# Layer 3 of a four-layer convolution network on one core: from halves to quarters of the channels

## The chip, the cores and the metric

The kernel runs on one core of one Trainium2 chip. Its time is device microseconds, the median of the runs. The core has a matrix engine (TensorE, PE in the profile, with its weight loads as PEld), a vector engine (VectorE, DVE), an activation engine (ScalarE, ACT), a general engine (GpSimd, POOL) and a queue engine (SyncE, SP) that here only issues transfers. Sixteen DMA engines move data between the main memory and the on-chip memory of 128 partitions. TensorE writes to PSUM, from which VectorE and ScalarE read.

## The reference

x has 16 images of 64 x 64 pixels with 256 channels, all in float32. Four layers follow one another, each x = x + layer(groupnorm(x)). Layer 0 is a linear attention, layer 1 a gated attention over channels and space with a scan, layer 2 an involution of 3 x 3, layer 3 an involution of 7 x 7. The change concerns layer 3 and what feeds it:

```
def _L3_conv_ref(x, w_reduce, gamma, beta, mean, var, w_span, b_span):
    K = 7; G = 16
    r = jnp.einsum('bhwc,cd->bhwd', x, w_reduce)
    r = jax.nn.relu((r - mean) * (gamma / jnp.sqrt(var + BN_EPS)) + beta)
    kgen = jnp.einsum('bhwd,de->bhwe', r, w_span) + b_span
    kgen = kgen.reshape(B, H, W, G, K * K)
    ...
    patches = jnp.stack([xp[:, i:i + H, j:j + W, :] for i in range(K) for j in range(K)], axis=3)
    patches = patches.reshape(B, H, W, K * K, G, Cg)
    out = jnp.einsum('bhwgk,bhwkgc->bhwgc', kgen, patches)
```

Each pixel has its own 49 weights for each of 16 groups of 16 channels. They are computed from the pixel (256 channels to 64, then to 784) and multiplied with the 7 x 7 neighbourhood.

## The kernel before

The four layers run one after the other over all images, each with pools of its own; images go between them through tensors in main memory.

Layer 2 (lines 882 to 1284) is written in an order by hand. One turn of its loop works on an eighth of an image for each of four tasks, which lie 0, 12, 20 and 33 turns behind (LAG): the end of layer 1, the projection, the involution itself, and `centred` (line 1174). The involution runs in 128 of the 161 turns. It writes its result as x3_d (tokens by channels, line 1136) and c3_d (channels by tokens). `load_centred` and `centred` take an eighth of x3_d back in the tile xc ([P, 8, P]: 8 rows of pixels and 128 channels, two buffers), subtract the channel means on POOL, and store it in sixteen transfers to `strips`. That tensor holds, for each half h of the channels, the padded image in eight strips of 14 columns (8 and three on each side), so that 9 rows of a strip are 126 consecutive rows. A turn's stores are issued in the following turn, all on SP; only in the last turns every second one goes by ACT (line 1229). The zero rows and columns of `strips` are written in layer 0, in `entered` (line 237), once an image.

Layer 3 (lines 1288 to 1492) goes over images, halves h of 128 channels, and eleven turns td. Here the framework's planner may move instructions on an engine, within what the data permits. At td = 0 `matrices(h)` (line 1353) makes four tiles wm, each for 32 channels, that is two groups: PE multiplies the spread weights `span` with the reduced pixels rt into a PSUM tile pk (three in turn, shared with pa), and ACT (line 1379, four instructions) or DVE (line 1384, one) adds the bias and moves it to wm. Five of twelve tiles go to ACT. Each wm has 126 rows, the places of a tile of 9 x 14 inputs, and for each of 176 tiles of 3 x 8 outputs 2 x 24 columns. There are four wm buffers, all in use by one half.

`involution7` (line 1420) is one turn: two rows of tiles, k, and eight tiles in each. For each tile four matmuls, one for each wm, multiply xw (the patches, 126 x 32) with wm into 32 partitions each of pa. Both groups' kernels are applied to all 32 channels; the instructions on ACT (line 1437) and DVE (line 1438) then take the right one with the mask msk and the norm's factor. `finished` (line 1443) transposes the turn before back to tokens on PE, adds the residual ot and stores it.

`load_patches` loads two xw of 512 KB (six buffers), two turns ahead; `load_residual` loads ot one turn ahead (three buffers). In a half with h = 1, each turn also reduces a part of the next image: `load_reduced` and `reduced` (line 1323), with four matmuls and three instructions on ACT. All transfers of layer 3 are issued on SP.

Of the kernel before, what the change touches and what calls it, by code (L numbers as in the profile page):

```python
# [44 lines left out]
def network(ctx: ExitStack, tc: tile.TileContext, a: dict, out: bass.AP):  # L45
# [21 lines left out]
    gmat = const("gmat", [P, P], a["gmat"])  # L67
    ones = const("ones", [P, P])
    nc.vector.memset(ones, 1.0)
# [24 lines left out]
    strips = dram.tile([NI, 2, HW + 9, TC + 6, NTC, P], F32, tag="strips", name="strips")  # L94
# [89 lines left out]
    with ExitStack() as st:  # L184
# [22 lines left out]
        hsum = aconst("hsum", [P, 4], a["hsum"])  # L207

# [28 lines left out]
        def entered(i, ch):  # L237

            if ch == 0:

                for h in range(2):
                    for r0, n in ((0, 3), (67, 6)):
                        nc.sync.dma_start(
                            out=strips[i, h, r0 : r0 + n].rearrange("r w t c -> (r w) (t c)"),
                            in_=a["zero"][0 : n * (TC + 6), :],
                        )
                    for tj, c0 in ((0, 0), (NTC - 1, TC + 3)):
                        nc.sync.dma_start(
                            out=strips[i, h, 3:67, c0 : c0 + 3, tj, :],
                            in_=a["zero"][0:HW, 0 : 3 * P].rearrange("r (w c) -> r w c", w=3),  # L250
                        )
# [630 lines left out]
    with ExitStack() as st:  # L882
# [61 lines left out]
        def load_centred(i, rc):  # L944
            q, h = divmod(rc, 2)
            x3n = x3_d[i].rearrange("(g r w) c -> g w r c", g=2, w=HW)
            load("xc", [P, 8, P], *(
                (
                    lambda t, g=g: t[g * HW : (g + 1) * HW],
                    x3n[g][:, q * 8 : q * 8 + 8, h * P : (h + 1) * P],  # L950
# [223 lines left out]
        def centred(i, rc):  # L1174


            q, h = divmod(rc, 2)
            xc = taken("xc")
            mean = gmb[i][:, h * P : (h + 1) * P]
            nc.gpsimd.tensor_tensor(  # L1180
                xc, xc, mean.unsqueeze(1).broadcast_to([P, 8, P]), ALU.subtract
            )
            for g in range(2):
                r0 = 3 + 32 * g + 8 * q
                for tj in range(NTC):
# [3 lines left out]
                        strips[i, h, r0 : r0 + 8, c0 : c0 + hi - lo, tj, :].rearrange(  # L1189
# [98 lines left out]
    with ExitStack() as st:  # L1288
        pc = st.enter_context(tc.tile_pool(name="c_const", bufs=1))
        wk = st.enter_context(tc.tile_pool(name="c_work", bufs=2))  # L1290
        wm_p = st.enter_context(tc.tile_pool(name="c_wm", bufs=4))
# [9 lines left out]
        wr3 = cconst("wr3", [P, 2, 64], a["w_reduce"].rearrange("(h p) f -> p h f", p=P))  # L1301
        wr3t = cconst("wr3t", [P, 2, 2, 64])
        for k in range(2):
            nc.vector.tensor_copy(wr3t[:, :, k, :], wr3)
# [48 lines left out]
        def matrices(h):  # L1353
# [3 lines left out]
            for q in range(4):  # L1357
                w = wm_p.tile([P, NTL, 2 * TILE_OUT], F32, tag="wm", name="wm")
                wm.append(w)
                for n in range(12):  # L1360
# [3 lines left out]
                    for m in range(2):  # L1364
                        for b in range(2):
# [5 lines left out]
                                lhsT=span[half, h * 8 + q * 2 + gg, s0 : s0 + P],  # L1371
# [95 lines left out]
        for n, (i, h, td) in enumerate(turns):  # L1467
# [13 lines left out]
            if td == 0:  # L1481
                wm = matrices(h)
# [118 lines left out]
```

## Time and profile before

| | us |
|---|---|
| median of 3 runs | 10119.68 (10116.0 to 10123.17) |
| profiled execution | 10143.46, its span 10141.2 |
| PE busy | 7922.7 (78%) |
| DVE busy | 6659.6 (66%) |
| ACT busy | 5277.9 (52%) |
| POOL busy | 2348.4 (23%) |
| patch matmuls, line 1428 | 45056 instructions, busy 826.8, idle before them 503.5 |
| matrix matmuls, line 1369 | 12288 instructions, busy 1186.3, idle before them 151.8 |
| bias on DVE, line 1384 | 896 of 1.343 us |
| bias on ACT, line 1379 | 2560 of 0.542 us |

Times in the views are microseconds from the start of one profiled execution. Busy time of an engine is an average over stages with different limits. A number in brackets behind an instruction is the time for which its engine stood idle before it, and what ended that; "issue" means that the profile shows no release. One matmul of the program appears as two instructions where its operands are float32. The DMA share is the mean busy share of the sixteen DMA engines.

### The profile page before, as it was taken

The numbers are of one execution on the slowest core, as the hardware profiler recorded it, in microseconds if no ns is written. First come the engines' busy times: TensorE is split into PE (matmuls) and PEld (weight loads), VectorE is DVE, ScalarE is ACT, GpSimd is POOL, SyncE is SP. The second block draws the span as 40 slices with busy tenths as digits, with TensorE's granted clock in tenths as the row PEclk, the third lists the DMA queues.
The fourth block names the chain that finished last, engine by engine and source line by source line (L and its number), as shares of the span: only waits on it lengthen the run. The fifth ranks groups of instructions, "written<-read, shape, count | busy, mean of one in ns | idle before, by whom it ended". The sixth has DMA issues, their size and how long they took to land.

```text
span 10141.2 us, 213891 instructions
## 1 busy us (share of the span) xinstructions
PE 7922.7 (78%) x85976; PEld 5657.2 (56%) x85976; DVE 6659.6 (66%) x11056; ACT 5277.9 (52%) x12544; POOL 2348.4 (23%) x1193
## 2 busy tenths in 40 slices
PE   8888888888888774777777777745787877777787
PEld 5666666666666531454554545533565656656565
DVE  4666666666666546799999999963454545545454
ACT  4555555555555436666666666533444444444444
POOL 0111111111110101567777677650000000000000
PEclk9999999999999868899889898967998888889988
DMA  7433444443343228667777777664656565555555
GB/s 244 143 131 127 136 142 140 135 133 129 127 145 115 86 82 262 203 209 229 228 229 228 228 227 229 192 152 137 206 165 196 163 203 168 180 183 183 185 163 189
DMA packets 1373248, 1762.68 MB, mean 174 GB/s; under 512 B 103649, under 2 KB 1067570, under 8 KB 1371106
## 3 DMA queue, kind: packets, MB, share of 16 engines
q1 hardware_dynamic: 1360266, 1743.26, 55.2%
q8 instruction: 679, 11.12, 0.4%
q10 hardware_dynamic: 11992, 5.74, 0.3%
q14 instruction: 311, 2.55, 0.1%
HBM read 1234.54 MB, written 536.87 MB: 175 GB/s over the span
## 4 chain that ended last, share of the span: by engine, by line
PE 33%; DVE 28%; DMA 13%; ACT 11%; issue 8%; POOL 4%; SPq 2%; ACTq 0%; DVEq 0%; POOLq 0%
DVE pd L1105 7%; PE pa L1428 7%; DVE wm L1384 6%; PE pq L296 5%; PE pk L1369 5%; PE py L452 4%; DMA x<-x_d 3%; PE pr L1337 3%; DVE x L1273 2%; DMA c_d<-c 2%; ACT sq L461 2%; ACT wm L1379 2%; DMA strips<-xc 2%; DMA xn<-x_d 2%; DVE y L457 1%
## 5 line engine op out<-in xcount | busy, mean ns | idle before, releaser
L296 PE MATMUL pq<-wq,xn 128*128 128x384 f32 x4096 | 1474.0, 499 | 62.3 <-DVE diag L345 20.9
L1105 DVE TENSOR_TENSOR pd<-xs,pw 128x576 f32<-128x576 f32 (+15 forms) x3072 | 1437.5, 546 | 8.9 <-PE pw L1059 5.5
L1369 PE MATMUL pk<-rt,span 64*128 64x176 f32 x12288 | 1186.3, 331 | 151.8 <-DVE wm L1384 60.0
L1384 DVE TENSOR_TENSOR wm<-pk,spanb 128x704 f32<-128x704 f32 x896 | 1148.3, 1343 | 229.2 <-PE pk L1369 229.2
L1428 PE MATMUL pa<-wm,xw 126*32 126x48 f32 x45056 | 826.8, 228 | 503.5 <-issue 405.8
L1369 PEld LDWEIGHTS pk<-rt,span 64*128 64x128 f32 x12288 | 949.7, 190 | 383.0 <-ACT wm L1379 181.9
L1116 POOL TENSOR_TENSOR pd<-pd 128x2048 f32<-128x2048 f32 (+2 forms) x384 | 1068.2, 2782 | 404.0 <-DVE pd L1105 383.9
L1379 ACT ACTIVATE wm<-pk,spanb 128x176 f32<-128x176 f32 x2560 | 976.2, 542 | 344.4 <-PE pk L1369 335.9
L1428 PEld LDWEIGHTS pa<-wm,xw 126*32 126x32 f32 x45056 | 686.6, 125 | 748.5 <-issue 549.2
L1438 DVE SCALAR_TENSOR_TENSOR ex<-pa,msk,ex 128x192 f32<-128x192 f32 x704 | 286.9, 415 | 1189.3 <-ACT ex L1437 1187.3
L296 PEld LDWEIGHTS pq<-wq,xn 128*128 128x128 f32 x4096 | 751.8, 193 | 495.5 <-issue 56.3
L1437 ACT ACTIVATE ex<-pa,msk 128x192 f32<-128x192 f32 x704 | 289.7, 421 | 1057.8 <-PE pa L1428 1055.1
L1075 PE MATMUL pt<-ident,pad 128*128 128x128 f32 x4608 | 637.5, 292 | 158.2 <-ACT rt L1052 54.6
L1028 PE MATMUL px<-x2p,wis 128*128 128x512 f32 x1024 | 571.5, 706 | 212.7 <-ACT c L1130 177.3
L1075 PEld LDWEIGHTS pt<-ident,pad 128*128 128x128 f32 x4608 | 540.6, 151 | 316.7 <-ACT rt L1052 66.3
L1079 ACT COPY xs<-pt 128x512 f32<-128x512 f32 x1152 | 607.8, 587 | 184.2 <-PE pt L1075 183.6
L1273 DVE TENSOR_REDUCE x<-pd 128x512 f32<-128x4608 f32 x128 | 633.3, 4948 | 1.4
L452 PE MATMUL py<-wo,oT 128*128 128x256 f32 x2048 | 486.6, 389 | 60.8 <-DVE va L312 45.2
L464 POOL TENSOR_TENSOR rsy<-ss,mhalf 128x4 f32<-128x4 f32 x128 | 130.1, 1017 | 1629.4 <-DVE ss L462 1629.4
L461 ACT ACTIVATE sq<-y 128x256 f32<-128x256 f32 x512 | 213.2, 416 | 526.0 <-DVE y L457 517.6
L1028 PEld LDWEIGHTS px<-x2p,wis 128*128 128x128 f32 x1024 | 217.4, 226 | 471.9 <-issue 230.9
L1344 ACT ACTIVATE rt<-pr,b,sb 128x128 f32<-128x128 f32 x528 | 202.0, 452 | 516.1 <-PE pr L1337 516.1
(242 smaller groups left out, 13899.4 us busy)
## 6 DMA issues: line engine op xcount, KB each, us to landing
xw<-strips SPq DMA_DIRECT2D x704, 512.0 KB
xn<-x_d SPq DMA_DIRECT2D x256, 512.0 KB
x<-x_d SPq DMA_DIRECT2D x256, 512.0 KB
x_d<-x SPq DMA_DIRECT2D x256, 512.0 KB
strips<-xc SPq DMA_DIRECT2D x1464, 56.0 KB
xin<-in_x SPq DMA_DIRECT2D x256, 256.0 KB
x_d<-xc SPq DMA_DIRECT2D x128, 512.0 KB
xm<-x_d SPq DMA_DIRECT2D x128, 512.0 KB
```

The source lines that it names most:

```text
L296: nc.tensor.matmul(pq[:, dd, 0:384], lhsT=xn[:, h, tok], rhs=wq[:, h, hf * 384 : (hf + 1) * 384], start=(h == 0), stop=(h == 1),)
L452: nc.tensor.matmul(py[:, q, :], lhsT=oT[hf][:, q * P : (q + 1) * P], rhs=wo[:, hf, :], start=(hf == 0), stop=(hf == 1),)
L1028: nc.tensor.matmul(px, lhsT=w[:, h, fh * P : (fh + 1) * P], rhs=x2[:, h], start=(h == 0), stop=(h == 1),)
L1075: nc.tensor.transpose(pt[:, k, h * P : (h + 1) * P], lines[:, h, rc * 4 + e + k, 2 * j : 2 * j + P], ident,)
L1079: nc.scalar.copy(t[:, e : e + 2, 0:C], pt)
L1105: nc.vector.tensor_tensor(pd[:, :, o - oh * P : o - oh * P + n, :], xs[dj][:, di : di + 4, c0 : c0 + 9 * n].rearrange("p r (f k) -> p r f ...
L1116: nc.gpsimd.tensor_tensor(pd[..., 0:n], pd[..., 0:n], pd[..., n : 2 * n], ALU.add)
L1273: nc.vector.tensor_reduce(x3[:, :, P:C], pd1, AX.X, ALU.add)
L1369: nc.tensor.matmul(pkv[:, b, m], lhsT=span[half, h * 8 + q * 2 + gg, s0 : s0 + P], rhs=rto[half, o, :], start=True, stop=True,)
L1379: nc.scalar.activation(dst[:, m // 2, m % 2], pkv[:, m // 2, m % 2], AF.Identity, bias=spanb[:, g0 + m : g0 + m + 1],)
L1384: nc.vector.tensor_tensor(dst, pkv, spanb[:, g0 : g0 + 4].rearrange("p (b m) -> p b m", b=2).unsqueeze(3).broadcast_to([P, 2, 2, NTL]), AL ...
L1428: nc.tensor.matmul(pav[32 * q : 32 * q + 32, :, tj * TC : (tj + 1) * TC], lhsT=xws[k][0:TILE_IN, tj, 32 * q : 32 * q + 32], rhs=wm[q][0:TI ...
```

## The change

Layer 3 goes over quarters of 64 channels (a half h and a part pr) and not over halves. For each quarter two matrices wm are made (two buffers, before four), and a turn of `involution7` puts its two rows of tiles k side by side in the partitions of one pa: 64k + 32q. A turn so has half of the matmuls that it had, one instruction on ACT and one on DVE, and there are twice as many turns. `finished` has two transposes of 96 columns.

The patches have 24 tiles xw of 4 KB a partition, each for one turn of a quarter. A quarter's eleven are loaded at the start of the quarter before. The residual ot has four buffers of 4 x 64, in blocks of 96 tokens by 64 channels. The tile that ends a quarter is handed to `finished` before the next matrices. ACT takes 4 and 5 of twelve PSUM tiles in turn.

`strips` is laid out by quarters, so xc is [P, 16, 64], 16 rows and 64 channels, and a stored or loaded piece is 64 channels long. The zero rows of all quarters go in one transfer each. The constants gmat and ones move to pools of earlier layers, wr3 is loaded straight into wr3t, and the mask is made with small matmuls.

```
-    strips = dram.tile([NI, 2, HW + 9, TC + 6, NTC, P], F32, tag="strips", name="strips")
+    strips = dram.tile([NI, 4, HW + 9, TC + 6, NTC, 64], F32, tag="strips", name="strips")
...
-                for h in range(2):
-                    for r0, n in ((0, 3), (67, 6)):
-                        nc.sync.dma_start(
-                            out=strips[i, h, r0 : r0 + n].rearrange("r w t c -> (r w) (t c)"),
-                            in_=a["zero"][0 : n * (TC + 6), :],
-                        )
+                for r0, n in ((0, 3), (67, 6)):
+                    nc.sync.dma_start(
+                        out=strips[i, :, r0 : r0 + n].rearrange("q r w t c -> q (r w) (t c)"),
+                        in_=a["zero"][:, 0 : n * (TC + 6), :],
+                    )
+                for q in range(4):
...
         def load_centred(i, rc):
-            q, h = divmod(rc, 2)
+            quarter, q = divmod(rc, 2)
...
-            load("xc", [P, 8, P], *(
+            load("xc", [P, 16, 64], *(
...
-                    x3n[g][:, q * 8 : q * 8 + 8, h * P : (h + 1) * P],
+                    x3n[g][:, q * 16 : q * 16 + 16, quarter * 64 : quarter * 64 + 64],
...
-                        strips[i, h, r0 : r0 + 8, c0 : c0 + hi - lo, tj, :].rearrange(
+                        strips[i, quarter, r0 : r0 + 16, c0 : c0 + hi - lo, tj, :].rearrange(
                             "r w c -> w r c"
...
-        wm_p = st.enter_context(tc.tile_pool(name="c_wm", bufs=4))
+        wm_p = st.enter_context(tc.tile_pool(name="c_wm", bufs=2))
+        xw_p = st.enter_context(tc.tile_pool(name="c_xw", bufs=NTR + 2))
...
-        def matrices(h):
+        def matrices(h, pr):
...
-            for q in range(4):
+            for q in range(2):
...
-                    if n % 12 in (1, 3, 6, 8, 10):
+                    if n in ((1, 4, 6, 9), (1, 3, 6, 8, 10))[q]:
...
+        TB = TR * HW // 2
...
+        def tokens(t, i, h, pr, td):
+
+            t = t[i, :, h * P + pr * 64 : h * P + pr * 64 + 64]
+            t0 = td * TR * HW
+            if t0 + 4 * TB <= NT:
+                return [t[t0 : t0 + 4 * TB].rearrange("(m p) c -> p m c", p=TB)]
...
+        def load_patches(i, quarter, td):
+
+            xw = xw_p.tile([P, 2, NTC, 64], F32, tag="xw", name="xw")
+            rows = strips[i, quarter].rearrange("r w t c -> (r w) (t c)")
+            t0, step = td * TR * (TC + 6), TR * (TC + 6)
+            for k in range(2):
                 nc.sync.dma_start(
+                    out=xw[:, k].rearrange("p t c -> p (t c)"),
+                    in_=rows[t0 + k * step : t0 + k * step + P],
+                )
+            xws[i, quarter, td] = xw
+
+        def load_residual(i, h, pr, td):
+            ot = wk.tile([P, 4, 64], F32, tag="ot", name="ot", bufs=4)
+            for dst, src in zip(blocks(ot, td), tokens(x3_d, i, h, pr, td)):
+                nc.sync.dma_start(out=dst, in_=src)
             return ot
...
+            for tj in range(NTC):
+                for k in range(2):
+                    for q in range(2):
+                        p0 = 64 * k + 32 * q
                         nc.tensor.matmul(
+                            pav[p0 : p0 + 32, :, tj * TC : (tj + 1) * TC],
+                            lhsT=xw[0:TILE_IN, k, tj, 32 * q : 32 * q + 32],
...
+            nc.scalar.activation(ex, pag[:, 0], AF.Identity, scale=msk[:, pr, h, 0:1])
+            nc.vector.scalar_tensor_tensor(
+                ex, pag[:, 1], msk[:, pr, h, 1:2], ex, ALU.mult, ALU.add
+            )
             return ex
...
+        def finished(i, h, pr, td, ex, ot):
+
+            po = sm.tile([P, 2, P], F32, tag="sm", name="po")
+            for b in range(2):
+                nc.tensor.transpose(po[0:TB, b, :], ex[:, b * TB : (b + 1) * TB], ident)
...
+            return list(zip(tokens(outs, i, h, pr, td), blocks(ot, td)))
...
             if td == 0:
+                if quarters:
+                    following = quarters.pop(0)
+                    for t in range(0, NTR, 2):
+                        load_patches(*following, t)
+                if last:
+                    for dst, src in finished(*last):
+                        nc.sync.dma_start(out=dst, in_=src)
+                    last = None
+                wm = matrices(h, pr)
+            ex = involution7(i, h, pr, td, wm, msk)
             if last:
                 store = finished(*last)
-            if h == 1 and i + 1 < NI:
+            if h == pr == 1 and i + 1 < NI:
                 reduced(i + 1, td, cs.pop((i + 1, td)))
```

## The prediction

> **What bounds it now.** I read the page first, for where the transfers are busy. One digit is 254 us. Layer 2's multiplications run from 4127 to 6749 us (digits 17 to 27, mostly 7), layer 3's matrices begin at 6956 us (digit 28 on, 5 and 6).
>
> ```profile
> DMA  7433444443343228667777777664656565555555
> ```
>
> Then the view by stretches, with two rounds of layer 3 cut into their two stages.
>
> ```profile
> 7961.00:7999.00 38.00, 33.72 (x366) 26.99 (x362) 33.43 (x28) 28.64 (x76) 0.00 (x0) 1.00 0.14 43
> 8000.00:8048.00 48.00, 34.57 (x1393) 26.77 (x1390) 14.44 (x32) 9.37 (x24) 0.00 (x0) 0.79 0.83 269
> 8050.00:8089.00 39.00, 33.95 (x364) 27.06 (x361) 34.06 (x29) 28.82 (x76) 0.00 (x0) 1.00 0.17 57
> 8090.00:8154.00 64.00, 48.92 (x1490) 33.22 (x1488) 15.88 (x38) 20.99 (x56) 0.00 (x0) 0.87 0.83 269
> ```
>
> The columns are us, then busy us and instructions of PE, weight loads, DVE, ACT and POOL, then granted clock, DMA share and GB/s. While matrices are made (38 and 39 us) the DMA share is 0.14 and 0.17; while they are used (48 us, or 64 with the next image's reduction) it is 0.83. The round is a sum of two stages with different limits: DVE, ACT and the ring of PSUM tiles in one, patches in the other. The order of time shows it in PE: it stands idle for "issue" in front of patch matmuls when buffers have run dry, and goes fast when they are full.
>
> ```profile
> 8031.73 1.23 PE L1428 MATMUL pa<-wm,xw 126*32 126x48 f32 x97 [2.15 <-issue]
> ...
> 8044.45 0.89 PE L1428 MATMUL pa<-wm,xw 126*32 126x48 f32 x64 [0.59 <-DVE ex L1438]
> 8045.27 0.33 PE L1449 MATMUL po<-ident,ex 128*128 128x128 f32 x1
> 8045.53 0.89 PE L1428 MATMUL pa<-wm,xw 126*32 126x48 f32 x64
> 8046.35 0.44 PE L1449 MATMUL po<-ident,ex 128*128 128x128 f32 x2
> ```
>
> The change also touches layer 2, which writes the strips. There DVE is bound (20.35 us a turn: two first multiplications lie at 5506.95 and 5527.30), and SP is hardly freer:
>
> ```profile
> 5505.77 9.61 SPq L1230 DMA_DIRECT2D strips<-xc  x16
> 5506.95 11.23 DVE L1105 TENSOR_TENSOR pd<-xs,pw 128x576 f32<-128x576 f32 x24
> ...
> 5517.27 1.29 SPq L926 DMA_DIRECT2D xc<-x_d  x2
> 5518.60 0.62 SPq L926 DMA_DIRECT2D x2p<-x_d  x1
> ...
> 5525.23 1.25 SPq L1230 DMA_DIRECT2D c_d<-c  x2
> ```
>
> SP spends 9.6 us on sixteen strip stores, then stands 1.9 us until they have landed, because the next xc goes into their buffer; everything else of its turn takes 8.2 us, so its loop is about 19.7 us.
>
> **The price of a packet.** Two stretches move nearly one size alone: the end of layer 2 (512-byte pieces) and layer 1's statistics (2 KB rows).
>
> ```profile
> 6800.00:6900.00 100.00, 0.00 (x0) 0.00 (x0) 0.00 (x0) 0.00 (x0) 21.04 (x9) 0.50 0.62 130
> ...
> 3830.00:3930.00 100.00, 66.66 (x112) 18.09 (x112) 78.72 (x225) 77.28 (x225) 0.00 (x0) 0.95 0.87 291
> ```
>
> The view of the DMA queues counts their packets:
>
> ```profile
> DMA packets 27686, 13.04 MB, mean 130 GB/s; under 512 B 2264, under 2 KB 27684, under 8 KB 27684
> ...
> DMA packets 15094, 29.14 MB, mean 291 GB/s; under 512 B 890, under 2 KB 890, under 8 KB 15088
> ```
>
> 0.62 x 16 engines x 100 us = 992 engine-us over 25,422 packets is 39 ns, 38 with something off for the small ones; 0.87 x 1600 over 14,204 is 98 ns. The straight line through them (0.039 ns a byte, 18 ns fixed) gives 178 ns for 4 KB, 78 for 1.5 KB, 28 for 256 B. Test on before: an image of layer 3 moves 5632 patch rows of 4 KB, 16,384 pieces of 512 B (residual in, result out) and 2816 of 1.5 KB: 1002 + 623 + 220 = 1845 engine-us, 115 us on 16 engines; the measured share is 0.56 of 198.5 us (3176 us over 16 images), 111. The line holds, but 256 B lies outside the two sizes.
>
> [...]here 64 patch instructions take 0.89 or 1.51 us, and the clock is 1.00 with matrices and 0.79 with patches.
>
> **Part by part.** Layer 3, matrices. A quarter makes 24 PSUM tiles. Before, 48 take 40.4 us (first at 6956.4, first patch matmul at 6996.8), 0.84 us each, and a changeover costs about 1.7 more (42.2 us from the last patch matmul at 8049.3 to full use at 8091.5). So a quarter: 20.3 + 1.7 = 22 us, an image 88 where it had 84. DVE gets 15 of 24 tiles, before 14. The three-tile ring, not DVE, sets the pace (PE waits for both engines' tiles), so I cost this at nothing; were DVE the bound, eight tiles of 1.34 us make 10.7 against 10.1 us in every other matrix, 0.6 x 64 = 38 us.
>
> Layer 3, patches. Their loads go out at a quarter's start, for the next: 22 x 128 rows of 2 KB = 2816 x 98 ns / 16 = 17 us, hidden by 22 us of matrices. Then PE: a turn has 64 instructions (0.89 us warm, four column groups as before) and two transposes (0.44, as the pair above): 1.33 us. The chain from a matmul through ACT (0.42) and DVE (0.42) to the transposes is 1.05 us (8043.4 to 8044.45), and the next turn's matmuls cover 0.89 of it and the earlier transposes the rest. At the mean clock of the two patch stretches, 0.83, the turn is 1.6; with 0.1 for waits I take 1.7 us, 18.7 a quarter; ends 1.33 and 2.2 (1.51 + 0.69, cold). The residual and the result, 8192 pieces of 256 B in a quarter at 28 ns on 16 engines, need 14.3 us and fit. The fourth quarter has the reduction: four matmuls of 1.56 us in a turn as now, 3.3 x 11 = 36 us. An image: 88 + 3 x 18.7 + 36 = 180 against 198.5: 18.5 x 16 = -296; I write -290. Its DMA work is 1104 + 918 + 220 = 2242 engine-us, 140 us: below 180. Ends: all warm 164 us, -550; all patch turns at 2.2, and 4 with the reduction, 205 us, +100. SP issues some 190 transfers an image instead of 99; at 0.33 to 0.6 us, 63 to 114 us: it stays free.
>
> The mask by four small matmuls once an image, the added DVE adds (22 of 256 elements for 11 of 384) and wr3's load without its two copies lie under matrices or DVE's idle time (14.4 busy of 48 us): nothing. Without that cover the mask would cost about 1 us an image.
>
> Layer 2. xc is read and the strips are written in pieces of 64 channels: 1024 + 1696 packets of 512 B become 5440 of 256 B a turn: 103 to 152 engine-us at 28 ns, +3.1 us. The DMA share there is 0.79 (16 us of 20.35), so 19.1 us, 94%. No issue is added: sixteen stores remain. But xc's reload waits for the stores: 1.9 us may become 3, SP's loop 20.8. I take 0.5 us over 128 turns, +64; below nothing is excluded, since DVE's work there is untouched. The last 13 turns, with nothing but this (11 us each), grow by 2: +26.
>
> Layer 0. The zero rows go out with the quarter as slowest dimension[...]. Loads queue behind them once an image. I take 1.3 us x 15 = +20; ends 0 and 9 x 15 = 135.
>
> Sum: -290 + 64 + 26 + 20 = -180 us. Against the profiled execution (span 10141.2, 10143.46 us in all) that is 9963; it lies 23.8 us above the median of the three runs, so for the median 10119.68 - 180 = 9940.
>
> **Rivals.** Slower: 256-byte packets bind layer 2. Point of decision: the turn's other packets take 156 engine-us, so 5440 packets fill 20.35 us at 31 ns; the whole gain is gone near 36. If a packet costs 38 ns whatever it holds, the turn is 22.7 us: +2.3 x 128 = 300, the tail +52; in layer 3 residual and result need 19.5 us a quarter, about 2 us a turn, an image 192: -105; with +20, +267: 10,390. For it: [...]DMA, SP and DVE within a few per cent of each other. Against: the line through three sizes.[...]
>
> Second: the patches are early, but residual and result take their place: four buffers, each to be loaded, used and stored before it comes round, on an in-order SP. At 2.1 us a turn an image is 88 + 69 + 41 = 198: no gain, and with +110 in layers 2 and 0 about 10,230. [...]Against: it is issued a turn ahead, and four buffers serve half as many bytes.
>
> Third: all warm, layer 2 unmoved: -550 + 46, about 9,620[...]. Against: a clock of 0.87 where PE was busy 49 of 64 us.
>
> **Chances.** Forecast (9,800 to 10,090) 0.51, slower by packets 0.29, residual 0.12, all warm 0.08. Range 9,700 to 10,400. A measurement here can tell 0.2%, 20 us, from no change. Faster: nearly all of the forecast and the third, 0.56; same 0.05; slower 0.39.
>
> **What would show it.** DMA share in the matrix stretches up from 0.15 to about 0.8; no idle "issue" of 1 to 3 us before patch matmuls; 1.3 to 2 us between two; clock 0.9 or more; layer 2's turn under 21 us, the wait of xc's load for the strips under 3 us. I am wrong if DVE's multiplications in layer 2 begin to wait and the turn is above 22 us, or if the result's transposes wait for residuals.

## The result, and the profile after

The changed kernel takes 10157.99 us (median of six runs, 10144.61 to 10161.18), the kernel before on the same chip 10120.62 us (10116.0 to 10145.18). The ratio is 1.0032, 95% interval 1.0019 to 1.0045: slower by about a third of a per cent, where 9940 us was forecast. The profiled execution took 10144.61 us with a span of 10142.8; the one before had a span of 10141.2. The medians differ by 37 us, these two traces by only 1.6, because the profiled execution of the changed kernel was the fastest of its six and that of the kernel before lies 23 us above its median. Inside, the traces differ by much more.

First the granted clock of PE in forty slices of 254 us, of the kernel before:

```profile
PEclk9999999999999868899889898967998888889988
```

and the clock and the DMA share of the changed kernel:

```profile
PEclk8898999999999977798988888886899999999999
DMA  5343443334443324758888888876766666666665
```

In the last third the DMA share is now an even 6 where stretches of 0.14 and 0.83 alternated: the patches do go beside the matrices. But three of the first four digits of the clock are lower, and the first digit of DMA fell from 7 to 5. That is layer 0, and it is where most of the gain went. The view of one tile says when its first and last instructions start. For the products `pd` of layer 2, of the kernel before:

```profile
L1105 DVE TENSOR_TENSOR pd<-xs,pw x3072: 177/576/755, 4126.9 to 6748.9; 128x576 f32<-128x576 f32 x64, 128x180 f32<-128x180 f32 x64, 128x360 f32<-128x360 f32 x64
```

and of the changed kernel:

```profile
L1106 DVE TENSOR_TENSOR pd<-xs,pw x3072: 184/584/765, 4287.7 to 6944.2; 128x576 f32<-128x576 f32 x64, 128x180 f32<-128x180 f32 x64, 128x360 f32<-128x360 f32 x64
```

The first `wm` eviction of layer 3, from the same view of `wm`, before and after:

```profile
L1384 DVE TENSOR_TENSOR wm<-pk,spanb x896: 1316/1344/1364, 6957.3 to 10086.3; 128x704 f32<-128x704 f32 x180
```

```profile
L1388 DVE TENSOR_TENSOR wm<-pk,spanb x960: 1315/1342/1365, 7155.8 to 10118.6; 128x704 f32<-128x704 f32 x192
```

With the spans, the kernel falls into four stretches:

| stretch | before, us | after, us | difference | forecast |
|---|---|---|---|---|
| layers 0 and 1, to the first `pd` | 4126.9 | 4287.7 | +161 | +20 |
| layer 2, first to last `pd` | 2622.0 | 2656.5 | +34.5 | +64 |
| tail of layer 2, to the first `wm` | 208.4 | 211.6 | +3 | +26 |
| layer 3, to the end | 3183.9 | 2987.0 | -197 | -290 |

The changed kernel by stretches (columns as in the prediction): first a stretch of layer 2, then from layer 3 a patch phase, a matrices phase and another patch phase.

```profile
5200.00:6200.00 1000.00, 737.06 (x3860) 503.52 (x3859) 943.84 (x1494) 621.39 (x1469) 690.38 (x336) 0.86 0.82 224
8014.00:8034.00 20.00, 13.19 (x718) 10.12 (x718) 6.89 (x19) 4.33 (x11) 0.00 (x0) 1.00 0.51 134
8036.00:8057.00 21.00, 18.52 (x192) 14.64 (x189) 19.34 (x18) 13.83 (x36) 0.00 (x0) 1.00 0.76 246
8112.00:8133.00 21.00, 15.47 (x696) 11.79 (x700) 7.33 (x18) 4.46 (x11) 0.00 (x0) 0.84 0.46 122
```

The matrices take about 22 us a quarter, as forecast, with a share of 0.76 beside them. The patch phase takes about 22 us, not 18.7, although the clock is 1.00 or 0.84 in these two and the DMA share has fallen from 0.83 to 0.5. The order of time on PE shows what is in it:

```profile
8017.43 0.74 PE L1446 MATMUL pa<-wm,xw 126*32 126x48 f32 x49
8019.97 0.38 PE L1446 MATMUL pa<-wm,xw 126*32 126x48 f32 x15 [1.80 <-issue]
...
8020.62 0.89 PE L1446 MATMUL pa<-wm,xw 126*32 126x48 f32 x64
...
8021.95 0.70 PE L1446 MATMUL pa<-wm,xw 126*32 126x48 f32 x43
8023.88 0.45 PE L1446 MATMUL pa<-wm,xw 126*32 126x48 f32 x21 [1.24 <-issue]
```

The idle "issue" is still there, and it doesn't stand where a patch would be waited for. It falls inside a turn and moves back through it: after 49 matmuls of the turn, then 43. From one stall to the next there are 15 + 64 + 43 matmuls and the transposes, 126 in all, every one with its weight load. Over all of layer 3 the counts from one stall to the next are 126, 127 or 128, or multiples of about 127. So in these traces the stalls go by a count of instructions, not by patches. The page counts 684 packets with 11.21 MB on the larger of two queues of the kind "instruction": 16.4 KB each. PE has 86488 matmuls and as many weight loads, 253 instructions for each packet, about what lies between two stalls. From this came the two questions of the experiments: what made layer 0 late, and what does PE wait for in layer 3.

### The profile page after: what moved, and what is told of

The parts are those of the page before. It is cut to its first block, busy times and chain, and to the rows that moved or that the text cites. A ratio compares the mean times of both kernels' runs of the same rounds, so it can differ in the third digit from the quotient of the medians.

```text
span 10142.8 us, 217765 instructions
## 1 busy us (share of the span) xinstructions
PE 7939.5 (78%) x86488; PEld 5609.8 (55%) x86488; DVE 6777.1 (67%) x11518; ACT 5190.7 (51%) x12288; POOL 2336.3 (23%) x1193
## 3 DMA queue, kind: packets, MB, share of 16 engines
q1 hardware_dynamic: 2087066, 1743.43, 58.2%
q8 instruction: 684, 11.21, 0.5%
## 4 chain that ended last, share of the span: by engine, by line
PE 30%; DVE 26%; DMA 14%; issue 11%; ACT 11%; POOL 4%; SPq 3%; DVEq 0%; POOLq 0%; ACTq 0%
DVE wm L1388 8%; PE pq L297 6%; DVE pd L1106 5%; PE pa L1446 5%; PE py L453 4%; PE pk L1373 4%; DMA c_d<-c 3%; DMA x<-x_d 2%; ACT sq L462 2%; DMA strips<-xc 2%; DVE x L1274 2%; PE po L1465 2%; DMA c<-c_d 2%; SPq L1231 2%; PE pr L1340 2%
## 5 line engine op out<-in xcount | busy, mean ns | idle before, releaser
L297 PE MATMUL pq<-wq,xn 128*128 128x384 f32 x4096 | 1503.2, 509 | 95.5 <-ACT xn L168 49.1
L1388 DVE TENSOR_TENSOR wm<-pk,spanb 128x704 f32<-128x704 f32 x960 | 1220.8, 1340 | 257.5 <-PE pk L1373 183.1
L1383 ACT ACTIVATE wm<-pk,spanb 128x176 f32<-128x176 f32 x2304 | 883.9, 539 | 590.9 <-PE pk L1373 513.0
L1446 PE MATMUL pa<-wm,xw 126*32 126x48 f32 x45056 | 745.8, 216 | 280.8 <-issue 231.3
L1446 PEld LDWEIGHTS pa<-wm,xw 126*32 126x32 f32 x45056 | 610.8, 116 | 511.8 <-issue 403.5
L1029 PE MATMUL px<-x2p,wis 128*128 128x512 f32 x1024 | 548.3, 681 | 168.0 <-ACT c L1131 137.3
L1473 DVE TENSOR_TENSOR ot<-po,ot 96x256 f32<-96x256 f32 (+2 forms) x768 | 287.5, 385 | 570.6 <-PE po L1465 524.5
L1050 PE MATMUL pr<-x2r,wrs 128*64 128x512 f32 x512 | 335.1, 791 | 224.4 <-DMA x2r<-x_d 207.9
```

The costliest lines, as they stand in the source:

```text
L297: nc.tensor.matmul(pq[:, dd, 0:384], lhsT=xn[:, h, tok], rhs=wq[:, h, hf * 384 : (hf + 1) * 384], start=(h == 0), stop=(h == 1),)
L1029: nc.tensor.matmul(px, lhsT=w[:, h, fh * P : (fh + 1) * P], rhs=x2[:, h], start=(h == 0), stop=(h == 1),)
L1383: nc.scalar.activation(dst[:, m // 2, m % 2], pkv[:, m // 2, m % 2], AF.Identity, bias=spanb[:, g0 + m : g0 + m + 1],)
L1388: nc.vector.tensor_tensor(dst, pkv, spanb[:, g0 : g0 + 4].rearrange("p (b m) -> p b m", b=2).unsqueeze(3).broadcast_to([P, 2, 2, NTL]), AL ...
L1446: nc.tensor.matmul(pav[p0 : p0 + 32, :, tj * TC : (tj + 1) * TC], lhsT=xw[0:TILE_IN, k, tj, 32 * q : 32 * q + 32], rhs=wm[q][0:TILE_IN, (t ...
```

## The experiments

**e1: the zero rows quarter by quarter.** The only part of the change in layer 0 besides constants is how the zero rows of `strips` are filled.

```diff
-                for r0, n in ((0, 3), (67, 6)):
+                for q, r0, n in [(q, r, n) for q in range(4) for r, n in ((0, 3), (67, 6))]:
                     nc.sync.dma_start(
-                        out=strips[i, :, r0 : r0 + n].rearrange("q r w t c -> q (r w) (t c)"),
-                        in_=a["zero"][:, 0 : n * (TC + 6), :],
+                        out=strips[i, q, r0 : r0 + n].rearrange("r w t c -> (r w) (t c)"),
+                        in_=a["zero"][q, 0 : n * (TC + 6), :],
                     )
```

> Edit to the changed kernel: the zero rows of a strip are written by one DMA for each quarter (16 x 1344 and 16 x 2688 floats[...]) instead of one DMA with the quarters as its outermost dimension (4 x 2 x 10752 and 4 x 3 x 14336). Nothing else. Theory A (the fill whose outermost dimension is 4 costs layer 0 its 161 us): layer 2's first multiplication back from 4288 us to 4110 to 4160, layers 2 and 3 as in the changed kernel, time about 9,995 us (9,970 to 10,030), faster than both. Rival B (layer 0 is late from the smaller pieces and the larger number of transfers in the fill): start of layer 2 still above 4250 us, time 10,140 to 10,200.

It took 9997.72 us, ratio to before 0.9861 (0.9844 to 0.9877), and `pd` says where:

```profile
L1106 DVE TENSOR_TENSOR pd<-xs,pw x3072: 177/578/758, 4129.4 to 6785.3; 128x576 f32<-128x576 f32 x64, 128x180 f32<-128x180 f32 x64, 128x360 f32<-128x360 f32 x64
```

Layer 2 begins at 4129.4, 158 us earlier, with four times as many transfers for the rows. So the fill with the quarters outermost cost 158 of the 161 us, and rival B falls. The fill can do so in two ways: the transfers hold up what is behind them, or the planner, which orders layer 0 as it does layer 3, lays the work out otherwise around them. The programs do differ in order: if PE's order is written down as runs of equal matmuls with their counts, the first 1300 entries of e1 differ from before in 80 lines, from the changed kernel in 386.

**e2 and e3: the same order, both forms.** The kernels from here to e8 below were timed in one execution each; stretches that an edit doesn't touch agree within 25 us. Layer 0's loop is kept in the order of the program text, in the changed kernel (e2) and in e1's (e3):

```diff
+        with tc.manual_schedule():
-        for ch in range(NCH):
-            load("xin", 0, ch)
+            for ch in range(NCH):
+                load("xin", 0, ch)
...
```

> The changed kernel with layer 0's work kept in the order in which the program writes it, instead of the planner's. The zero rows go through the DMA with outermost dimension 4, as in the changed kernel. It is one half of a pair: only its difference from the next run counts. Theory H (the fill itself holds up the transfers behind it): layer 2 begins 80 us or more later than in the next run. Theory P (the planner takes the fill for long and puts layer 0 in a worse order around it): the two begin layer 2 within 30 us of one another.

> The same fixed order of layer 0 with the zero rows written by one DMA for each quarter. Order of the compute engines in layer 0 is that of the run before. Theory H: layer 2 begins 80 to 160 us earlier than in the run before. Theory P: within 30 us of it, and what the changed kernel lost is then the order that the planner chose.

**e9 and e10: the same with four times the dose.** Three more fills go into spare memory. Both have the same orders of PE, DVE and ACT and as many transfers; e10's transfers have 16 as their outermost dimension. First the edit of e9 to e2, then that of e10 to e9.

```diff
+                    for t in [strips[i]] + [spare[i, k] for k in range(3)]:
+                        t = t[:, r0 % 64 : r0 % 64 + n] if len(t.shape) and t.shape[1] == 9 else t[:, r0 : r0 + n]
...
```

```diff
-                            out=t.rearrange("q r w t c -> q (r w) (t c)"),
+                            out=t.rearrange("q r w t c -> q (r w t c)").rearrange("q (p x) -> p q x", p=16),
...
```

> The fixed order of layer 0 again, with each zero-row fill made four times: once into the strips and three times into spare memory that nothing reads. All in the form with outermost dimension 4. Its partner is the next run. Theory H[...]: layer 2 begins 300 us or more later than in the next run. Theory P (a fill costs layer 0 about 1 us): later by no more than 100 us.

> The same four fills in the same fixed order of all engines and with the same number of DMAs and bytes, each DMA with 16 as its outermost dimension (16 x 4 x 1344 and 16 x 4 x 2688). Theory H: layer 2 begins 300 us or more before the run before. Theory P: at most 100 us before it, and within 60 us of the single fill's 5314 us.

The first and last `pd`, in order of e2, e3, e9, e10:

```profile
L1107 DVE TENSOR_TENSOR pd<-xs,pw x3072: 178/578/756, 5328.6 to 7977.9; 128x576 f32<-128x576 f32 x64, 128x180 f32<-128x180 f32 x64, 128x360 f32<-128x360 f32 x64
```

```profile
L1107 DVE TENSOR_TENSOR pd<-xs,pw x3072: 177/576/754, 5314.1 to 7967.3; 128x576 f32<-128x576 f32 x64, 128x180 f32<-128x180 f32 x64, 128x360 f32<-128x360 f32 x64
```

```profile
L1110 DVE TENSOR_TENSOR pd<-xs,pw x3072: 175/578/757, 5432.3 to 8088.0; 128x576 f32<-128x576 f32 x64, 128x180 f32<-128x180 f32 x64, 128x360 f32<-128x360 f32 x64
```

```profile
L1110 DVE TENSOR_TENSOR pd<-xs,pw x3072: 177/576/755, 5330.5 to 7989.8; 128x576 f32<-128x576 f32 x64, 128x180 f32<-128x180 f32 x64, 128x360 f32<-128x360 f32 x64
```

One dose costs 14.5 us, which a single run hardly tells from nothing; four cost 101.8, a hair over the 100 set for theory P and far under the 300 of H: 25 us for a dose of 16 images, 1.6 us an image. The fills are as dense there as in the changed kernel: the 64 of e9 go out over 4129 us, the 16 of the changed kernel over 1053, about 65 us for each. So the form as such is worth 15 to 25 us of the 161 in this order. But these kernels are slow in layer 0 (layer 2 begins at 5314 us in e3), so the price holds for an order in which PE has slack.

That the rest is order is argued from the traces of the changed kernel, e1 and the kernel before. The loss lies in the first 1100 us: the changed kernel's 1176th matmul of `pq` starts 177 us later than that of before, the last of the 4096 164 us later. The views of waits over this stretch (us in all, times, longest); ScalarE and VectorE before,

```profile
ACT qa L304 <- PE pq L296: 103.6, 72, 5.6
ACT xn L169 <- DMA xn<-x_d: 61.1, 40, 3.1
```

```profile
DVE va L312 <- ACT ka L308: 100.7, 70, 5.6
DVE xn L170 <- DMA xn<-x_d: 61.7, 46, 3.2
```

and in the changed kernel:

```profile
ACT qa L305 <- PE pq L297: 218.0, 89, 5.6
ACT xn L168 <- DMA xn<-x_d: 39.6, 20, 4.2
```

```profile
DVE va L313 <- ACT ka L309: 230.8, 94, 7.5
DVE xn L169 <- DMA xn<-x_d: 27.8, 18, 3.6
```

Were loads held up behind the fills, the waits for loads would have grown. With PE's waits for `xin` (29.5 us before, 41.3 after) the three make 152 us before and 109 after, while the engines' waits for one another doubled. The order of time at one changeover of layer 0 shows why. In the changed kernel:

```profile
126.77 0.38 PE L157 MATMUL pv<-gn_d,gmat 128*128 128x2 f32 x2 [1.06 <-DVE gn_d L154]
129.83 0.47 PE L342 MATMUL pk<-ident,mx 128*128 128x128 f32 x1 [2.67 <-DVE mx L327]
132.56 0.79 PE L349 MATMUL pb<-diag,ones 128*128 128x128 f32 x2 [2.26 <-DVE diag L346]
138.02 9.14 PE L360 MATMUL pctx<-va,ka 128*128 128x129 f32 x64 [4.67 <-DVE ka L352]
```

and the same step in e1:

```profile
112.86 0.36 PE L157 MATMUL pv<-gn_d,gmat 128*128 128x2 f32 x2
113.17 0.91 PE L297 MATMUL pq<-wq,xn 128*128 128x384 f32 x2
115.01 0.91 PE L297 MATMUL pq<-wq,xn 128*128 128x384 f32 x2 [0.93 <-DVE xn L169]
115.76 0.27 PE L342 MATMUL pk<-ident,mx 128*128 128x128 f32 x1
115.87 2.75 PE L297 MATMUL pq<-wq,xn 128*128 128x384 f32 x8
118.45 0.38 PE L349 MATMUL pb<-diag,ones 128*128 128x128 f32 x2
```

The small matmuls of the changeover (pv, pk, pb) wait for DVE between one another. In e1 projections `pq` stand between them in PE's order; in the changed kernel nothing does, and PE idles. In the first 1100 us it makes 1176 `pq` there and 1380 before. The order of SP shows what the planner moved: before, the last row fill stands behind 52 loads of `xin` and 28 of `xn` and goes out at 286.3 us, in e1 behind 52 and 31 at 337.3 us; in the changed kernel it stands behind 98 and 73 and goes out at 1052.6 us. These are places in the order of SP's instructions, and a slow transfer does not change them. The loss ends with the fills: while they last, the first `xin` loads of successive images lie 251 to 259 us apart in the changed kernel, afterwards 216 to 227, and in the kernel before about 218 from the fourth image on. That alone would fit either theory.

**e5: the same transfers from another queue.** The row fills are issued on ScalarE's queue, so that the planner sees something else.

```diff
-                    nc.sync.dma_start(
+                    nc.scalar.dma_start(
                         out=strips[i, :, r0 : r0 + n].rearrange("q r w t c -> q (r w) (t c)"),
```

> The changed kernel with the two zero-row fills of each image issued by ScalarE's queue instead of SyncE's. They keep their form with outermost dimension 4, so the transfers are those of the changed kernel; the planner, which sees another queue, orders layer 0 otherwise. Theory P (the order of layer 0 cost the time, the transfers as such some 15 us as in the fixed pair): layer 2 begins between 4130 and 4180 us, of which up to 20 us are ScalarE's 32 issues of 0.6 us. Rival H[...]: layer 2 begins after 4250 us as in the changed kernel.

Layer 2 begins at 4404.1 us. Theory P as written missed; rival H's mark, after 4250 us, is met, though layer 2 begins 116 us later still than in the changed kernel. The waits in the first 1100 us, of ScalarE and VectorE:

```profile
ACT xn L168 <- DMA xn<-x_d: 93.0, 39, 4.7
ACT xc L262 <- DMA strips<-in_zero: 63.1, 1, 63.1
ACT L262 <- DMA strips<-in_zero: 34.7, 1, 34.7
```

```profile
DVE xn L169 <- DMA xn<-x_d: 207.6, 44, 11.9
```

The first fills stand ahead of ScalarE's first copies, which waited 98 us for them; and the rest followed by 512 us instead of 1053. Now the loads are late: 207.6 us of VectorE's waits for `xn` against 27.8. By these waits fills with four outermost can hold up loads when they come close together. The run doesn't decide between P and H, since it changed order and density at once, but it shows what H looks like in the waits, and the changed kernel, whose waits for loads are below those of before, doesn't look like it. The changed kernel's own order with another form of fill was not run.

**e4: half the patch instructions, in the kernel before.**

```diff
-                    for q in range(4):
+                    for q in range(2):
                         nc.tensor.matmul(
-                            pav[32 * q : 32 * q + 32, :, tj * TC : (tj + 1) * TC],
-                            lhsT=xws[k][0:TILE_IN, tj, 32 * q : 32 * q + 32],
-                            rhs=wm[q][0:TILE_IN, (td + k) * NTC + tj, :].rearrange(
+                            pav[64 * q : 64 * q + 64, :, tj * TC : (tj + 1) * TC],
+                            lhsT=xws[k][0:TILE_IN, tj, 64 * q : 64 * q + 64],
+                            rhs=wm[2 * q][0:TILE_IN, (td + k) * NTC + tj, :].rearrange(
...
```

> The kernel before with the patch matmuls of layer 3 made two at a time: 64 columns of weights for each instead of 32, so half as many matmuls and weight loads in that phase; transfers, buffers and evictions as before. Each pair of 32 channels is computed with the first one's matrix, so one matrix of two is made and left unused. Theory F (PE waits for its own instructions[...]): the waits that the profile puts down to issue come every second turn instead of every turn, and layer 3 falls from 3184 us by 130 us or more. Rival T (the transfers of patches bound the phase): layer 3 within 40 us of 3184.

**e6: the same in the changed kernel.**

```diff
-                    for q in range(2):
-                        p0 = 64 * k + 32 * q
-                        nc.tensor.matmul(
-                            pav[p0 : p0 + 32, :, tj * TC : (tj + 1) * TC],
+                    nc.tensor.matmul(
+                        pav[64 * k : 64 * k + 64, :, tj * TC : (tj + 1) * TC],
...
```

> The changed kernel with its patch matmuls two at a time: 64 columns of weights for each instead of 32, so 32 matmuls and 32 weight loads in a turn instead of 64 and 64; transfers and evictions as before. 64 channels are computed with one matrix instead of two (tile k with matrix k, the other half of each matrix is unused). Theory F (PE's instruction fetch): the waits put down to issue before the patch matmuls, 223 us in the changed kernel, go to below 60, and layer 3 falls from 2987 us by 80 us or more, although the 32 matmuls themselves take longer (1.14 us in the wide kernel before against 0.89 for the 64). Rival T (transfers bound the turn): layer 3 within 40 us of 2987, with waits for patches or residuals in place of issue.

e4: 9960.35 us, layer 3 from 6964.8 to 9958.6, 2994 us: 190 less, with every transfer in place. e6: 9925.42 us, layer 3 2747 us: 240 less. PE's waits in layer 3, each kernel's line for patch matmuls; before and e4:

```profile
PE pa L1428 <- issue: 405.8, 243, 5.1
```

```profile
PE pa L1428 <- DVE ex L1438: 162.9, 176, 1.0
...
PE pa L1428 <- DMA xw<-strips: 22.5, 32, 1.7
```

The changed kernel and e6:

```profile
PE pa L1446 <- issue: 231.3, 191, 3.0
```

```profile
PE pa L1444 <- issue: 0.8, 1, 0.8
```

With half the patch instructions "issue" is gone from both, though 32 wide matmuls take longer (1.14 us) than 64 narrow ones (0.89). Only 22.5 us of PE's waits for patches remain in e4. Theory F holds in both, though in e4 it had expected a stall every second turn and there is none; the rival holds in neither. The queue of 16.4 KB packets, in e4 and e6:

```profile
q8 instruction: 504, 8.26, 0.3%
```

```profile
q8 instruction: 508, 8.32, 0.4%
```

Before and in the changed kernel it carried 679 and 684. Both edits take out 22528 matmuls and as many weight loads, and 175 and 176 packets went with them: 257 and 256 instructions to a packet. On these counts the packets go with PE's instructions, 256 or so to each, and PE's idle "issue" before patch matmuls went with them: 405.8 us to none in e4, 231.3 to 0.8 in e6.

A rival is that SP, which stands 320 us for stored results in layer 3 of the changed kernel, holds the loads back. Eight residual buffers instead of four (e7) were to tell, but the patches take 96 KB a partition and 92.2 KB were left, so there is no time of that kernel. e6 answers in part: with the same four buffers the waits for issue are gone.

**e8: the patches loaded once.** Does the supply of instructions suffer from the loads beside it? The page of the changed kernel books both on the sixteen DMA engines: 58.2% of their time to the larger queue of data, 0.5% to the 684 packets of the kind "instruction". Theory L puts the pace down to the loads.

```diff
-            xw = xws.pop((i, 2 * h + pr, td))
+            xw = xws[0, 0, td]
...
-                    for t in range(0, NTR, 2):
+                    for t in range(0, 0, 2):
                         load_patches(*following, t)
```

> The changed kernel with patches loaded for the first quarter alone: all other quarters compute from those same patches, so some 470 MB of loads are left out of layer 3; PE's instructions, evictions, residual loads and stores stay. Theory L (PE's instruction fetch is slow[...]): the waits put down to issue fall from 231 us to below 90 and layer 3 from 2987 us by 120 us or more. Rival C (the fetch delivers 16 KB in some 4 us whatever the load): issue stays above 170 us and layer 3 falls by less than 60 us.

10059.07 us; layer 3 2907 us, 80 less. (The loads left out are 364 MB by the page's counts, not the 470 of the expectation.) A patch phase by stretches, and PE's waits in layer 3:

```profile
8089.00:8109.00 20.00, 12.97 (x702) 9.92 (x690) 7.13 (x19) 4.21 (x10) 0.00 (x0) 1.00 0.34 76
```

```profile
PE pa L1446 <- issue: 220.0, 203, 2.1
```

"issue" stays at 220 us with 364 MB of loads gone: theory L falls, and rival C is right on it; 80 us is outside both figures for the layer. With no loads behind it SP cannot hold any back, so the rival of the stored results falls too. The order of time gives the pace itself, as the mean time over layer 3 between two stalls with 122 to 134 matmuls between them: 5.27 us before (166 cases), 4.16 in the changed kernel (117), 3.90 in e8 (144), where a patch phase has a DMA share of 0.84, 0.51 and 0.34. So the supply was slower under the heaviest load (5.27 us at 0.84), but at less than half of that load (0.34) 128 matmuls still took three quarters of the time. What sets the 3.9 us was not tried.

**e11 to e13: using the pace that is left.** Where nothing else holds it, PE makes 24 matrix matmuls in 2.06 us, so 128 in 11 us, but 128 patch matmuls in 1.8. Mixing the two should even this out; the matrices of the next quarter go between the patch turns of the first three quarters, on the basis of e1.

```diff
-        wm_p = st.enter_context(tc.tile_pool(name="c_wm", bufs=2))
-        xw_p = st.enter_context(tc.tile_pool(name="c_xw", bufs=NTR + 2))
+        wm_p = st.enter_context(tc.tile_pool(name="c_wm", bufs=4))
+        xw_p = st.enter_context(tc.tile_pool(name="c_xw", bufs=7))
...
+            for t in order[n + 5 : n + 5 + 1]:
+                load_patches(*t)
...
-                wm = matrices(h, pr)
+                for _ in making or matrices(h, pr):
+                    pass
+                wm = made.pop((h, pr))
+                making = matrices(*divmod(2 * h + pr + 1, 2)) if 2 * h + pr < 3 else None
...
+            for _ in range(2 + td // 2 % 2 * (td < 8)):
+                if making:
+                    next(making, None)
```

> The kernel of e1 (zero rows by quarter) with four matrix buffers instead of two and seven patch buffers instead of twenty-four: two or three of the 24 steps that make the next quarter's two matrices are put after each patch turn of the first three quarters of an image, and patches are loaded five turns ahead. All of the computation is made. Layer 0 and layer 2 keep e1's order. Theory C (PE gets its instructions at some 4 us for every 128 matmuls and weight loads, and a matrices phase, which needs one such piece in 11 us, leaves that unused): a quarter's 920 matmuls need 7.2 pieces, 29 us, its evictions on VectorE 15 x 1.34 + 11 x 0.8 = 29 us, so 30 to 35 us instead of 42; three quarters of four over 16 images save 340 to 570 us, and the time is 9,430 to 9,660 us. Rival T (the loads of patches and the stores, now packed into less time, bound the phase): 9,900 us or more.

It was slower than both kernels: 10291.49 us, ratio 1.0156 (1.0137 to 1.0175). Theory C missed, and the time is past rival T's mark of 9,900 us. "issue" is nearly gone, as expected, but VectorE now waits for residuals. PE's and VectorE's waits in layer 3:

```profile
PE pa L1448 <- issue: 44.2, 39, 4.0
```

```profile
DVE ot L1475 <- DMA ot<-x_d: 629.7, 317, 4.8
```

e12 gives the residuals more room, and takes one buffer and one turn of lead from the patches:

```diff
-        xw_p = st.enter_context(tc.tile_pool(name="c_xw", bufs=7))
+        xw_p = st.enter_context(tc.tile_pool(name="c_xw", bufs=6))
...
-            ot = wk.tile([P, 4, 64], F32, tag="ot", name="ot", bufs=4)
+            ot = wk.tile([P, 4, 64], F32, tag="ot", name="ot", bufs=7)
...
-        res = [load_residual(*turns[0])]
+        res = [load_residual(*t) for t in turns[0:2]]
...
-            for t in order[n + 5 : n + 5 + 1]:
+            for t in order[n + 4 : n + 4 + 1]:
```

> The kernel of e11 with seven residual and result buffers instead of four, residuals loaded two turns ahead instead of one, three buffers instead of two for the reduced tensor and its loads two turns ahead, and six patch buffers with loads four turns ahead. All of the computation is made. Theory R (in e11 the residual's load waited in SyncE's queue for a stored result of three turns before, VectorE stood at the residual in the order of its queue, and the evictions behind it held PE): VectorE's waits for residuals go below a quarter of e11's, three quarters of an image take 30 to 36 us each and the time is 9,450 to 9,750 us. Rival E (work of both phases on the same three PSUM buffers and evictions in one order hold each other up, whatever the loads): 9,950 us or more.

10145.13 us, ratio 0.9999 (0.9988 to 1.0011): 146 us less than e11, still outside theory R's range and above the 9,950 of rival E. The residuals come in time now (20.6 us of VectorE's waits) and the patches don't; their shorter lead may be a part of that:

```profile
PE pa L1448 <- DMA xw<-strips: 305.2, 288, 3.4
```

e13 takes the patch loads out of SyncE's queue and gives the turn of lead back:

```diff
-                nc.sync.dma_start(
+                nc.gpsimd.dma_start(
                     out=xw[:, k].rearrange("p t c -> p (t c)"),
...
-            for t in order[n + 4 : n + 4 + 1]:
+            for t in order[n + 5 : n + 5 + 1]:
```

> The kernel of e12 with the patch loads issued by GpSimd's queue instead of SyncE's, five turns ahead. All of the computation is made. Theory Q (in e12 the patches stood in SyncE's queue behind residuals and stores that waited for earlier transfers to end, 977 us of waits, and PE waited 305 us for patches): PE's waits for patches go below 80 us and the time is 9,500 to 9,850 us. Rival G (GpSimd's issues, two a turn, are too slow for turns of 3 us, or the transfers as such are): PE's waits for patches stay above 200 us and the time is 10,000 us or more.

9959.07 us, ratio 0.9826 (0.981 to 0.9843). PE's waits for patches are gone, as theory Q has it, but the time is not in its range, nor in that of rival G. Which of the two edits did it, the queue or the lead, was not parted. Residuals are late again,

```profile
DVE ot L1475 <- DMA ot<-x_d: 336.9, 175, 5.9
```

and the reduced tensor is late as it was in e11 and e12 (226.3 us of PE's waits, 204.3 and 178.6 there). Each step moved the wait to another load; the estimate of 30 to 35 us a quarter left out that the loads must come at the same faster pace. e1 and e13 are both faster than the kernel before and the changed one; the two were not measured side by side. In their profiles layer 3 takes 3004 us in e1 and 2956 in e13, so the mixing was worth little of the 340 to 570 hoped for.

## Why the prediction was wrong

Its sum was -290 + 64 + 26 + 20 = -180 us; the traces have -197 + 34.5 + 3 + 161 = +1.5. Two terms failed, two were too dark.

**Layer 0, the term that turned the sign.** The step read "I take 1.3 us x 15 = +20", for loads that queue behind a fill; the 1.3 us was the author's estimate, and no trace of the kernel before showed it. As a price of the transfers that was about right: 1.6 us an image in e9 against e10. Yet the measured 161 lies above even its upper end of 135. The step that failed is that it put at nothing what the planner does: layer 0 has no order written out by hand, and after this edit SP's and PE's instructions came in another order. e1 shows that the edit of the fill cost 158 us. The pairs put 15 to 25 us of that on the transfers; that the other 135 us or so are the order is argued from the waits and from SP's sequence, and not shown by a run that keeps the planner's order and changes the form alone. Why the planner answers to the form was not looked into. The prediction treated an edit in a planned stretch as if only the edited instruction changed. With this term at zero the time would have been e1's, 9998 us.

**Layer 3, the patch turn.** "I take 1.7 us, 18.7 a quarter" came out as 2.0 and about 22: three such phases in 16 images are 3 x 3.3 x 16 = 158 us too much hope. The fourth quarter took 31.4 us on average instead of 36, which gives back 74, and all between the patch phases 89.2 an image instead of 88, which costs 19. The net is 103 us; the whole stretch, -197 for -290, shows 93. The step that failed lies earlier, in reading the profile: "it stands idle for 'issue' in front of patch matmuls when buffers have run dry". The buffers had not run dry. e4 shows 22.5 us of waits for patches once the instructions are halved, and e8 leaves the idle time where it was with no patches to load. On the counts between the stalls (126 to 128 matmuls) and to a packet (256 and 257 instructions) PE was waiting for its instructions, and of the signs named the idle "issue" did not go: earlier patches could help only as far as a lighter DMA load goes with a faster supply (5.27 and 4.16 us for 128 matmuls). The waits for issue before patch matmuls fell from 405.8 to 231.3 us, 174 of the 197 us that layer 3 gained; that the supply's pace is the link is argued from these numbers. Nor was the clock the limit: it was 1.00 in a phase that took some 20 us all the same.

**Layer 2.** At its tail the price of a packet was right; in the changed kernel,

```profile
7000.00:7100.00 100.00, 30.61 (x72) 15.31 (x72) 1.62 (x9) 12.59 (x33) 16.93 (x8) 0.57 0.70 135
```

```profile
DMA packets 41905, 13.46 MB, mean 135 GB/s; under 512 B 39243, under 2 KB 41903, under 8 KB 41903
```

0.70 x 1600 engine-us over 41905 packets is 27 ns, against 28 drawn from the line. In the turns themselves it was too high. The stretch shown of the changed kernel above (share 0.82) was before:

```profile
5200.00:6200.00 1000.00, 735.27 (x3930) 511.46 (x3931) 949.61 (x1521) 633.16 (x1497) 708.48 (x343) 0.90 0.78 227
```

From 0.78 to 0.82 is some 17 engine-us a turn (0.82 x 16 x 20.75 less 0.78 x 16 x 20.48), where the sum had 49 and a share of 0.94; which packets cost less than the line says is open. The turn grew by 34.5 / 128 = 0.27 us instead of 0.5, and the tail by 3 us instead of 26. VectorE's own work, busy for 944 of 1000 us, went on setting the pace, and the xc reload's waits for strips were 200.8 us where they had been 191.0.

**The rivals.** The packets' 38 ns did not come: they took 27 at the tail of layer 2. The residual ring did not bind in the changed kernel (VectorE's waits for residuals and stored results are 22.7 and 16.8 us in layer 3), but it did in e11 (629.7 us for residuals), once turns were packed closer. "All warm" asked for 1.33 us a turn; 128 matmuls, two turns, took 4.16 us from one stall to the next. None of the three named a loss in layer 0.

## What to carry to other kernels

Where a planner orders a stretch, compare the order of every engine before and after an edit there, however small, before pricing it by its own duration. Before calling idle time before an instruction a wait for data, count the instructions between two stalls: here the count was constant (126 to 128 matmuls), half as many and wider matmuls took the wait away (231.3 to 0.8 us in e6), and leaving 364 MB of loads out did not (220.0 us in e8). When one wait is removed from a chain of loads in one queue, price the next load at the new pace first.

## What the runs showed of the hardware

- In layer 3 PE made about 128 matmuls with their 128 weight loads from one stall to the next, every 3.90 us at a DMA share of 0.34 (e8), 4.16 at 0.51 (changed kernel) and 5.27 at 0.84 (before). The 48-column patch matmuls (64 in 0.89 us) outran this; the 176-column ones (24 in 2.06 us) didn't. The profile books these stalls as "issue": 405.8 us before, 231.3 in the changed kernel. The "instruction" packets of 16.4 KB went with the instructions: 45056 instructions fewer were 175 and 176 packets fewer in e4 and e6.
- At the tail of layer 2 packets that were mostly of 256 bytes took 27 ns each, close to the 28 of the line through larger sizes; in the turns of layer 2 they added some 17 engine-us a turn where that line has 49.
- A fill of about a megabyte with an outermost dimension of 4 cost layer 0 1.6 us more on average than with 16 when such fills were spread over the stage in the fixed order (e9, e10); in e5, with the fills on ScalarE's own queue, that engine's first copies waited 98 us for the first of them.
